# Softmax denominators in a two-layer graph attention kernel: from a ones-matmul per head pair to block transposes, row sums and one small matmul per visit

## The chip, the cores and the metric

The kernel runs on 1 core of one Trainium2 chip. The metric is the device time of one execution in microseconds. Lower is better. The median before the change is 3263.24 us over 3 runs.

## What is computed

64 graphs of 256 nodes, 512 features each, go through two layers of masked attention over the adjacency matrix, each with a layer norm and a ReLU in front and a residual. Layer 0 has 4 heads of 64, layer 1 has 8 heads of 64.

```python
# layer 0
h = maximum(layernorm(x), 0)
q, k, v = split_heads(h @ Wq), split_heads(h @ Wk), split_heads(h @ Wv)
sim = where(adj, q k^T * 64**-0.5, -big);  attn = softmax(sim, over the keys)
x = x + (attn v) @ Wo + bo
# layer 1
h = maximum(layernorm(x), 0);  h = layernorm(h) * gamma + beta
q, k, v = split(h @ w_qkv.T)                      # 8 heads
scores = where(adj | eye, q k^T * 64**-0.5, -1e9)
x = x + (softmax(scores) v) @ w_out.T + b_out
```

What matters here is the softmax. The kernel takes exponentials without subtracting a maximum, multiplies the unnormalised exponentials with v, sums the exponentials over the keys by another way, and multiplies the product with the inverse of that sum. The change is in how that sum is made and how its inverse reaches the place where it is used.

## The kernel before, in words

**Steps and graphs.** A step `s` handles 2 graphs (G = 2), so there are 32 steps. The steps are software-pipelined: while step s is in its layer 1, step s+1 finishes layer 0 and step s+2 starts it. All activations are fp32. The products by weights are 2x2 block products in 7 multiplications (Strassen-like), so that each projection is a "set" of 7 products, numbered n = 1 to 7, taken in the order 1, 6, 5, 2, 7, 3, 4 (`SET`, at the end of the schedule). The result of a product lies in a bank of PSUM and is taken out ("evacuated") by one add of VectorE or one copy of ScalarE (`evacuate`, lines 732 to 749).

**Four shared banks.** `mm_tile` hands out four PSUM banks in turn. `bank_of` (line 783) lets two products share one bank: product 2 accumulates on top of product 1, product 3 on top of 5, and product 4 on top of 7, each after the first of the two was evacuated. The matmuls of product 4 can thus not start before the evacuation of product 7 (line 743) has read the bank.

```python
    SHARED = {2: 1, 4: 7, 3: 5}
```

**Pairs and visits.** Two heads of 64 make a pair (`pr`): 2 pairs in layer 0, 4 in layer 1, 192 in all. A "visit" works on two pairs at once (a few at the edges of the program on one). In the steady state there are three visits in a period of one step, at the places 2.0 (`AT_X`), 4.5 (`AT_Q0`) and 6.2 (`AT_Z`) of a period 6.4 long. A visit closes the two pairs of the visit before it and opens two new ones:

- close: `key_sums` (line 996) multiplies the exponentials, already added over the two halves of the keys by GpSimd (`key_halves`, line 951, result `pd`), with a 128x32 matrix of ones, so that each of four groups of 32 partitions of a bank holds the sums of one (graph, head) repeated 32 times. `invert` (line 1022) takes the reciprocal of that bank (VectorE, 2 instructions of 128x128 for each pair), guards its extremes (line 1032) and issues 8 DMAs for each pair that spread the 32 copies over the 64 partitions of a head (line 1041). `weigh_out` multiplies exponentials and v on TensorE and copies the product out by ScalarE; `normalise` (line 1044) multiplies it by the spread inverses on GpSimd.
- open: `scores` (TensorE), `mask_scores` (VectorE), `exponentials` (ScalarE), `key_halves` (GpSimd).

After each visit TensorE goes on with a projection set: after X the values of layer 1 (`project_v1`), then the output product of layer 0 and the second query/key set of layer 1 ("set B", places 3.5 to 4.5); after Q0 the query/key set of layer 0 and its values; after Z the first query/key set of layer 1 and the output product of layer 1.

**What sets the order.** The order of the instructions on TensorE, VectorE, ScalarE and GpSimd is written out by hand: `at(period, place, fn, ...)` puts every step into a list of events, the list is sorted by place, and each engine gets its instructions in that order. Every engine works through its own queue in order, so an instruction that waits holds all that stand behind it on that engine. The DMAs are issued on SP's queue, in order too, except a few at the edges of the program.

**Lines that the change and the prediction touch.** `norm1` and `norm1_rest` (lines 624 and 641) take the statistics of layer 1's two norms with `bn_stats` (line 576). `turn_blocks` (line 683) transposes 32x32 blocks of the activations on VectorE (line 686), and `move_blocks` (line 693) sends them by 16 DMAs to their places. `neighbours` (line 506) takes a maximum over each row of the adjacency matrix, `neighbours_out` and `neighbours_in` send those by way of DRAM to all partitions.

Of the kernel before, what the change touches and what calls it, by code (L numbers as in the profile page):

```python
# [8 lines left out]
FP = mybir.dt.float32  # L9
# [4 lines left out]
ALU = mybir.AluOpType  # L14
# [301 lines left out]
def fast_path(  # L316
# [19 lines left out]
    nc = tc.nc  # L336
# [3 lines left out]
    G = 2  # L340
# [39 lines left out]
    ones = const.tile([P, 32], FP, name="ones")  # L380
    nc.vector.memset(ones, 1.0)
    mhalf = const.tile([P, NT], FP, name="mhalf")
    nc.gpsimd.memset(mhalf, -0.5)

# [518 lines left out]
    def scores(s, lyr, pr, second):  # L903
        st = S[s]
        qk = st.pop(("qk", lyr, pr))

        sc = [
            [mm_tile([P, NIC, N]) if second and g == 0 else ps_sc.tile([P, NIC, N], FP, name="sc") for e in range(2)]
            for g in range(G)
        ]  # L910
        if second and sums_bank:
            tag = sums_bank.pop()
            banks.remove(tag)
            banks.append(tag)
        for g in range(G):
            for kc in range(NIC):
                for e in range(2):
                    rows = slice(e * DH, (e + 1) * DH)
                    k0 = g * N + kc * P
                    nc.tensor.matmul(  # L920
                        sc[g][e][:, kc, :], qk[rows, 1, k0:k0 + P],
                        qk[rows, 0, g * N:(g + 1) * N], start=True, stop=True,
                    )
# [12 lines left out]
        pd = sm.tile([P, 2, G, N], FP, name="pd", bufs=2)  # L936
        st["sc", lyr, pr], st["p", lyr, pr] = sc, (p, pd)

    def mask_scores(s, lyr, pr, g):

        st = S[s]
        sc, (p, pd), neg = st["sc", lyr, pr][g], st["p", lyr, pr], st[f"n{lyr}"]
        for e in range(2):
            nc.vector.tensor_tensor(p[e][:, g], sc[e], neg[:, :, g, :], ALU.add)  # L944

    def exponentials(s, lyr, pr, g):
        p, pd = S[s]["p", lyr, pr]
        for e in range(2):
            nc.scalar.activation(p[e][:, g], p[e][:, g], AF.Exp, scale=SCALE)  # L949

    def key_halves(s, lyr, pr, e):
        p, pd = S[s]["p", lyr, pr]
        nc.gpsimd.tensor_tensor(pd[:, e], p[e][:, :, 0, :], p[e][:, :, 1, :], ALU.add)  # L953


    def place_values(s, lyr):
        st = S[s]
        tile_o = act.tile([P, NB, HP1, N], FP, name="oT")
        if lyr:
            st["oT1"] = tile_o  # L960
            st["invb"] = [tile_o[:, 3], tile_o[:, 4]]
            st["inv"] = [tile_o[:, 6, i] for i in range(2)]
        else:
            flat = tile_o.rearrange("p b c n -> p (b c) n")
            st["oT0"] = flat[:, :NB].rearrange("p (b c) n -> p b c n", c=HP0)
            st["invb"] = [flat[:, 8:10], flat[:, 10:12]]
            st["inv"] = [flat[:, 12 + i] for i in range(2)]

    def weigh(s, lyr, pr):
        st = S[s]  # L970
        p, _ = st["p", lyr, pr]
        po = ps_sc.tile([P, G, N], FP, name="sc")
        for g in range(G):
            for kc in range(NIC):
                for r0 in range(0, P, 32):
                    nc.tensor.matmul(  # L976
                        po[r0:r0 + 32, g, :],
                        st[f"v{lyr}"][:, g * NIC + kc, pr * P + r0:pr * P + r0 + 32],
                        p[r0 // DH][:, g, kc, :], start=(kc == 0), stop=(kc == NIC - 1),
                    )  # L980
# [15 lines left out]
    def key_sums(s, lyr, prs):  # L996

        st = S[s]
        bank = mm_tile([P, 2, N])
        sums_bank[:] = [banks[-1]] if len(prs) > 1 else []  # L1000
        for i, pr in enumerate(prs):
            _, pd = st["p", lyr, pr]
            st["sums", lyr, pr] = bank[:, i]
            for g in range(G):
                for e in range(2):
                    r0 = 32 * (2 * g + e)
                    nc.tensor.matmul(  # L1007
                        bank[r0:r0 + 32, i, :], ones, pd[:, e, g, :], start=True, stop=True,
                        skip_group_check=True,
                    )  # L1010

    def inverse_places(s, lyr, pr, i):

        if (s, lyr) != (NSTEP - 1, 1):
            return S[s]["inv"][i], S[s]["invb"][i]
        if pr == 0:
            invb = wqk0[:, 6].rearrange("p c k o -> p (c k o)").rearrange("p (g n) -> p g n", g=G)
        else:
            invb = act.tile([P, G, N], FP, name="invb", tag=("n0", "ne", "ab")[pr - 1])
        return bo_b[:, i * N:(i + 1) * N], invb  # L1020

    def invert(s, lyr, pr, i, halves=(0, 1)):
        st = S[s]
        sums = st["sums", lyr, pr]
        if 0 in halves:
            st["place", lyr, pr] = inverse_places(s, lyr, pr, i)
        inv, invb = st["place", lyr, pr]
        for k in halves:
            nc.vector.reciprocal(inv[:, k * P:(k + 1) * P], sums[:, k * P:(k + 1) * P])  # L1029
        if 1 not in halves:  # L1030
            return
        nc.vector.tensor_tensor_reduce(
            out=sums, in0=sums, in1=inv, scale=1.0, scalar=0.0, op0=ALU.add, op1=ALU.max,
            accum_out=extremes[:, units[0]:units[0] + 1],
        )
        units[0] += 1
        for g in range(G):
            for e in range(2):
                r0 = 32 * (2 * g + e)
                for d0 in range(e * DH, (e + 1) * DH, 32):  # L1040
                    nc.sync.dma_start(invb[d0:d0 + 32, g, :], inv[r0:r0 + 32, :])  # L1041
        st["invb", lyr, pr] = invb

    def normalise(s, lyr, pr):
        dst, invb = S[s].pop(("dst", lyr, pr)), S[s].pop(("invb", lyr, pr))
# [27 lines left out]
    def visit(period, w, prev, cur):  # L1073
# [2 lines left out]
        s, lyr, prs = prev  # L1076
        last = (s, lyr) == (NSTEP - 1, 1)
        if prs:
            at(period, w, key_sums, s, lyr, prs)
            if prs[0] == 0 and not last:  # L1080
                at(period, w, place_values, s, lyr)
            for i, pr in enumerate(prs):
                k = i if len(prs) > 1 else pr % 2
                at(period, w + 0.1 * last, invert, s, lyr, pr, k, (0,) if i and not last else (0, 1))
                if not last:
                    at(period, w, weigh_out, s, lyr, pr)
                    at(period, w + (0.55 if len(prs) == 1 else (0.3, 0.75)[i]), normalise, s, lyr, pr)
        for i, pr in enumerate(cur[2]):
            unit = (*cur[:2], pr)
            one = cur[:2] == (0, 0)  # L1090
            at(period, w, scores, *unit, i == 1)
            at(period, w, mask_scores, *unit, 0)
            if i == 1 and len(prs) > 1 and not last:
                at(period, w, invert, s, lyr, prs[1], 1, (1,))
            at(period, w + 1 / 7 if one else w, mask_scores, *unit, 1)
            for g, place in enumerate((0.05, 0.22) if one else ((0.02, 0.03), (0.15, 0.3))[i]):
                at(period, w + place, exponentials, *unit, g)
            for e, place in enumerate((0.23, 0.3) if one else ((0.1, 0.11), (0.35, 0.36))[i]):
                at(period, w + place, key_halves, *unit, e)

    AT_X, AT_C0, AT_QK, AT_Q0, AT_V0, AT_H1, AT_Z = 2.0, 3.0, 3.5, 4.5, 5.5, 6.06, 6.2
    LAST_QK = 4.0
# [22 lines left out]
    visit(-1, 1.54, none, (1, 0, (1,)))  # L1125
    for s in range(NSTEP):

        p = s - 2
# [126 lines left out]
def kernel(tc, *args):  # L1255
# [1 line left out]
    B, N, _ = args[0].shape  # L1257
    P = 128
    with tc.tile_pool(name="guard", bufs=1) as guard:
        extremes = guard.tile([P, B // 2 * 6], FP, name="extremes")  # L1260
# [44 lines left out]
```

## Time and profile before

The numbers are of the one profiled execution, unless said otherwise.

| what | value |
|---|---|
| median of 3 runs (range) | 3263.24 us (3262.0 to 3267.05) |
| the profiled execution's own time | 3261.14 us |
| its span, first to last instruction | 3259.3 us |
| granted TensorE clock | 0.999 |
| TensorE busy (matmul) | 3204.8 us (98%) |
| VectorE busy | 2095.1 us (64%), 3680 instructions |
| ScalarE busy | 1256.6 us (39%) |
| GpSimd busy | 2241.4 us (69%) |
| length of a period in the middle (1413.76 to 1513.97, from one X visit to the next) | 100.2 us |

How to read it: a line of the profile with groups gives the line of the code, the engine, the operation, "output<-input", the shape, how many there were, then the busy time, the mean duration of one in ns, and after the second bar the idle time of the engine just ahead of them with what ended it. A timeline gives the start, the length and the engine of instructions in order, with the idle time ahead of them in brackets. A list of waits gives who waited for whom: the total, the number of times, and the longest.

### The profile page before, as it was taken

What the parts mean: (1) busy time and instruction counts of PE and PEld (TensorE: products, weight loads), DVE (VectorE), ACT (ScalarE), POOL (GpSimd) and SP (SyncE); (2) the same over time, 40 slices, a digit from 0 to 9 for tenths busy, and PEclk for the clock granted to TensorE, in tenths of its full rate; (3) what the DMA queues carried; (4) which work ended last, traced back from release to release, by engine and by line L of the source; (5) the groups of instructions that cost most, each with busy time, mean ns of one, the idle gap of its engine ahead of it and who ended that gap; (6) DMA issues with size and microseconds to landing.
All of it is one profiled execution on the core that took longest, in us unless ns stands there. A gap on an engine that the chain in (4) does not pass through costs nothing.

```text
span 3259.3 us, 59763 instructions
## 1 busy us (share of the span) xinstructions
PE 3204.8 (98%) x22002; PEld 2611.8 (80%) x22002; DVE 2095.1 (64%) x3680; ACT 1256.6 (39%) x2226; POOL 2241.4 (69%) x2124
## 2 busy tenths in 40 slices
PE   9999999999999999999999999999999999999999
PEld 6787878888887888788787888888787888878777
DVE  6656666666666666676666666666666666666665
ACT  4434343343433334343434334343333434343431
POOL 7776776777766767667677677776776766767653
PEclk9999999999999999999999999999999999999999
DMA  4122232232322322223223222222232222322211
GB/s 147 43 85 77 55 85 65 79 82 53 85 69 73 88 60 71 76 67 86 76 55 85 62 82 81 53 84 66 75 86 62 72 70 73 86 72 57 85 31 47
DMA packets 214217, 237.04 MB, mean 73 GB/s; under 512 B 75032, under 2 KB 128416, under 8 KB 213920
## 3 DMA queue, kind: packets, MB, share of 16 engines
q1 hardware_dynamic: 213488, 232.76, 26.0%
q8 instruction: 177, 2.90, 0.4%
q14 instruction: 120, 0.98, 0.1%
q10 hardware_dynamic: 432, 0.40, 0.0%
HBM read 86.12 MB, written 33.62 MB: 37 GB/s over the span
## 4 chain that ended last, share of the span: by engine, by line
PE 66%; POOL 13%; DVE 11%; DMA 5%; SPq 4%; issue 1%; ACT 0%; POOLq 0%; DVEq 0%; ACTq 0%
PE mm L803 26%; PE mm L860 12%; PE sc L976 9%; PE mm L830 7%; PE sc L920 6%; DVE bs L576 5%; SPq L1041 4%; PE mm L1007 3%; POOL xt L498 3%; DMA xt<-in_x_dram 2%; POOL xt L771 2%; POOL n L563 2%; PE mm L920 2%; DVE p L944 2%; DMA oT<-oT 2%
## 5 line engine op out<-in xcount | busy, mean ns | idle before, releaser
L803 PE MATMUL mm<-hT,wqkv 128*128 128x256 f32 x3584 | 795.7, 381 | 31.7 <-DVE qk L743 31.7
L803 PEld LDWEIGHTS mm<-hT,wqkv 128*128 128x128 f32 x3584 | 675.7, 190 | 144.8 <-DVE qk L743 43.7
L953 POOL TENSOR_TENSOR pd<-p 128x512 f32<-128x512 f32 x383 | 479.7, 1274 | 328.1 <-ACT p L949 327.6
L860 PE MATMUL mm<-wo,oT 128*128 128x256 f32 x2632 | 588.3, 381 | 7.6 <-POOL oT L412 5.2
L860 PEld LDWEIGHTS mm<-wo,oT 128*128 128x128 f32 x2632 | 498.9, 191 | 87.1 <-issue 8.8
L1029 DVE RECIPROCAL oT<-mm 128x128 f32<-128x128 f32 x376 | 345.6, 940 | 249.6 <-PE mm L1007 245.6
L949 ACT ACTIVATE p<-p 128x512 f32<-128x512 f32 x766 | 439.6, 626 | 137.0 <-DVE p L944 137.0
L944 DVE TENSOR_TENSOR p<-sc,n 128x512 f32<-128x512 f32 x579 | 363.5, 684 | 113.9 <-PE sc L920 112.5
L844 PE MATMUL mm<-wqkv,hT 128*128 128x256 f32 x1792 | 401.9, 382 | 0.0
L803 PE MATMUL mm<-hT,wqk 128*128 128x256 f32 x1792 | 398.9, 382 | 0.3 <-ACT qk L737 0.2
L803 PEld LDWEIGHTS mm<-hT,wqk 128*128 128x128 f32 x1792 | 338.2, 191 | 56.3 <-issue 10.7
L844 PEld LDWEIGHTS mm<-wqkv,hT 128*128 128x128 f32 x1792 | 335.5, 190 | 53.8 <-issue 10.7
L976 PE MATMUL sc<-p,v 128*32 128x256 f32 x6128 | 350.0, 379 | 1.0 <-issue 1.0
L976 PEld LDWEIGHTS sc<-p,v 128*32 128x32 f32 x6128 | 199.7, 110 | 132.9 <-issue 1.8
L988 ACT COPY oT<-sc 128x512 f32<-128x512 f32 x188 | 109.4, 582 | 500.2 <-PE sc L976 495.3
L1046 POOL TENSOR_TENSOR oT<-oT 128x512 f32<-128x512 f32 x188 | 240.0, 1277 | 83.2 <-DMA oT<-oT 73.5
L920 PE MATMUL sc<-qk 64*128 64x256 f32 x2320 | 292.6, 385 | 0.0
L920 PEld LDWEIGHTS sc<-qk 64*128 64x128 f32 x2320 | 218.7, 186 | 58.8 <-issue 39.6
L771 POOL TENSOR_TENSOR xt<-xt,u 128x512 f32<-128x512 f32 x183 | 228.9, 1272 | 4.4 <-DVE xt L760 1.9
L830 PE MATMUL mm<-wv,hT 128*128 128x256 f32 x1024 | 227.0, 379 | 0.4 <-DVE qk L747 0.4
L830 PEld LDWEIGHTS mm<-wv,hT 128*128 128x128 f32 x1024 | 194.2, 190 | 27.3 <-DVE qk L747 0.7
L592 ACT ACTIVATE h<-h,mr,r 128x512 f32<-128x512 f32 x252 | 184.6, 804 | 0.0
(139 smaller groups left out, 3781.8 us busy)
## 6 DMA issues: line engine op xcount, KB each, us to landing
h<-blocks SPq DMA_DIRECT2D x960, 64.0 KB, 2.0
oT<-oT SPq DMA_DIRECT2D x1504, 32.0 KB, 1.9
xt<-in_x_dram SPq DMA_DIRECT2D x31, 1024.0 KB, 5.8
h<-in_x_dram SPq DMA_DIRECT2D x31, 1024.0 KB, 5.5
out_dram<-xt SPq DMA_DIRECT2D x31, 1024.0 KB, 4.5
ne<-row SPq DMA_DIRECT2D x30, 256.0 KB, 4.7
ad<-in_adj_dram SPq DMA_DIRECT2D x32, 128.0 KB, 8.7
wr<-in_L_gnn_w_qkv_dram SPq DMA_DIRECT2D x3, 1024.0 KB, 9.2
```

Source lines behind the costliest of these rows:

```text
L771: (nc.vector if last else nc.gpsimd).tensor_tensor(r, r, u, ALU.add)
L803: nc.tensor.matmul(bank[:, k, :], w[:, wa, c, k, a * P:(a + 1) * P], st["hT"][:, ba, c, :], start=first and (k, c) == (0, 0), stop=(k, c) ...
L830: nc.tensor.matmul(bank, st["hT"][:, b0 + t // NIC * step, c % HC, i:i + P], wv0[:, c, :], start=(c == 0), stop=(c == NC - 1),)
L844: nc.tensor.matmul(bank[:, t, :], st["hT"][:, ba, c, t * P:(t + 1) * P], wqkv1[:, wa, c, 2, :], start=first and (t, c) == (0, 0), stop=(t, ...
L860: nc.tensor.matmul(bank[:, t, :], oT[:, ba, c, t * P:(t + 1) * P], w[:, wa, c, :], start=first and (t, c) == (0, 0), stop=(t, c) == (NIC - ...
L920: nc.tensor.matmul(sc[g][e][:, kc, :], qk[rows, 1, k0:k0 + P], qk[rows, 0, g * N:(g + 1) * N], start=True, stop=True,)
L944: nc.vector.tensor_tensor(p[e][:, g], sc[e], neg[:, :, g, :], ALU.add)
L949: nc.scalar.activation(p[e][:, g], p[e][:, g], AF.Exp, scale=SCALE)
L953: nc.gpsimd.tensor_tensor(pd[:, e], p[e][:, :, 0, :], p[e][:, :, 1, :], ALU.add)
L976: nc.tensor.matmul(po[r0:r0 + 32, g, :], st[f"v{lyr}"][:, g * NIC + kc, pr * P + r0:pr * P + r0 + 32], p[r0 // DH][:, g, kc, :], start=(kc ...
L1029: nc.vector.reciprocal(inv[:, k * P:(k + 1) * P], sums[:, k * P:(k + 1) * P])
L1046: nc.gpsimd.tensor_tensor(dst, dst, invb, ALU.mult)
```

## The change

Four things change together.

1. Sums over keys. `key_sums` no longer multiplies `pd` by ones. A new step `key_quarters` follows GpSimd's `key_halves` for each pair: VectorE transposes the 32x32 blocks of `pd` (one instruction of 128x1024), then sums along rows (one reduction from 128x1024 to 128x32, into `part`). At the next visit one matmul with `part` as the stationary matrix (128x64 for two pairs) and a 128x32 matrix of four identities (`quarters`) adds the four groups of 32 partitions. Its result is 64x32, each sum once.
2. Inverses. One reciprocal and one guard of 64x32 stand for the two pairs of a visit, in place of four reciprocals of 128x128 and two guards of 128x256. The inverses go to a line in DRAM by one DMA, and come back by two DMAs for each pair, each to 64 partitions with the same 2 KB for all.
3. Buffers. `pd` has one buffer in place of two, so GpSimd's `key_halves` of a pair waits until VectorE has transposed the pair before. `turned_p`, `part` and `inv` have one each.
4. Places. The statistics of layer 1's norms (`norm1`, `norm1_rest`) move from 3.7 to 3.82 and 3.95 to 4.2 to places between 3.79 and 4.37, spread among the evacuations of set B. The guard's array is cleared once at the start.

```diff
     def key_halves(s, lyr, pr, e):
-        p, pd = S[s]["p", lyr, pr]
-        nc.gpsimd.tensor_tensor(pd[:, e], p[e][:, :, 0, :], p[e][:, :, 1, :], ALU.add)
+        st = S[s]
+        p = st["p", lyr, pr]
+        if e == 0:
+            st["pd"] = sm.tile([P, 2, G, N], FP, name="pd", bufs=1)
+        nc.gpsimd.tensor_tensor(st["pd"][:, e], p[e][:, :, 0, :], p[e][:, :, 1, :], ALU.add)
+
+    def key_quarters(s, lyr, prs, i):
+
+        st = S[s]
+        if i == 0:
+            st["part", lyr, prs] = stat.tile([P, 2, 32], FP, name="part", bufs=1)
+        turned = sm.tile([P, 32, 32], FP, name="turned_p", bufs=1)
+        nc.vector.transpose(
+            turned, st.pop("pd").rearrange("p e g (b k) -> p (e g b) k", k=32),
+        )
+        nc.vector.tensor_reduce(st["part", lyr, prs][:, i], turned, axis=mybir.AxisListType.X, op=ALU.add)
...
     def key_sums(s, lyr, prs):
...
-        bank = mm_tile([P, 2, N])
+        part = st.pop(("part", lyr, prs))
+        rows = 32 * len(prs)
+        bank = mm_tile([P, 32])
         sums_bank[:] = [banks[-1]] if len(prs) > 1 else []
-        for i, pr in enumerate(prs):
-            _, pd = st["p", lyr, pr]
-            st["sums", lyr, pr] = bank[:, i]
-            for g in range(G):
-                for e in range(2):
-                    r0 = 32 * (2 * g + e)
-                    nc.tensor.matmul(
-                        bank[r0:r0 + 32, i, :], ones, pd[:, e, g, :], start=True, stop=True,
-                        skip_group_check=True,
-                    )
...
-        for k in halves:
-            nc.vector.reciprocal(inv[:, k * P:(k + 1) * P], sums[:, k * P:(k + 1) * P])
...
+        sums = bank[:rows]
+        nc.tensor.matmul(
+            sums, part[:, :len(prs)].rearrange("p i b -> p (i b)"), quarters, start=True, stop=True
+        )
+        inv = stat.tile([P, 32], FP, name="inv", bufs=1)[:rows]
+        nc.vector.reciprocal(inv, sums)
         nc.vector.tensor_tensor_reduce(
             out=sums, in0=sums, in1=inv, scale=1.0, scalar=0.0, op0=ALU.add, op1=ALU.max,
-            accum_out=extremes[:, units[0]:units[0] + 1],
+            accum_out=extremes[:rows, units[0]:units[0] + 1],
         )
         units[0] += 1
-        for g in range(G):
+        line = dram.tile([len(prs), 2, T], FP, name="line")
+        nc.sync.dma_start(line.rearrange("i e (b q) -> (i e b) q", q=32), inv)
+        for i, pr in enumerate(prs):
+            invb = inverse_place(s, lyr, pr, i if len(prs) > 1 else pr % 2)
             for e in range(2):
-                r0 = 32 * (2 * g + e)
-                for d0 in range(e * DH, (e + 1) * DH, 32):
-                    nc.sync.dma_start(invb[d0:d0 + 32, g, :], inv[r0:r0 + 32, :])
-        st["invb", lyr, pr] = invb
+                nc.sync.dma_start(
+                    invb[e * DH:(e + 1) * DH].rearrange("p g n -> p (g n)"),
+                    bass.AP(tensor=line.tensor, offset=line[i, e, 0:1].offset, ap=[[0, DH], [1, T]]),
+                )
+            st["invb", lyr, pr] = invb
...
+        late = w > AT_Z - 0.01 and period < NSTEP - 2
...
+            if cur[:2] == (1, 0):
+                at(period, w + 0.112, key_quarters, *cur[:2], (0, 1), pr)
+            else:
+                place = 0.31 if one else (0.34, 0.78)[i] if late else (0.29, 0.58)[i]
+                at(period, w + place, key_quarters, *cur, i)
...
-            at(p, ((2.901, 3.041, 3.181, 3.321), (2.99919, 2.99933, 2.99947, 2.99961), (3.7, 3.72, 3.8, 3.82))[edge][k], norm1, s, k)
+            at(p, ((2.901, 3.041, 3.181, 3.321), (2.99919, 2.99933, 2.99947, 2.99961), (3.79, 3.8, 3.94, 3.95))[edge][k], norm1, s, k)
             at(
-                p, ((3.042, 3.182, 3.322, 3.323), (2.99948, 3.2, 3.3, 3.45), (3.95, 4.02, 4.09, 4.2))[edge][k],
+                p, ((3.042, 3.182, 3.322, 3.323), (2.99948, 3.2, 3.3, 3.45), (4.08, 4.22, 4.23, 4.37))[edge][k],
                 norm1_rest, s, k,
             )
```

In VectorE's queue of the changed program, between the masks of a visit and the evacuation of product 7, there now stand, in this order:

- X: evacuation 6; first transpose and sum; evacuation 5; two `turn_blocks`; second transpose and sum; two `turn_blocks`; evacuation 7
- Q0: two `turn_blocks`; evacuation 6; first transpose and sum; two `turn_blocks`; evacuation 5; second transpose and sum; evacuation 7
- Z: first transpose and sum; evacuations 6 and 5; one `bn_stats` with its aggregation; second transpose and sum; one `neighbours`; evacuation 7

The two second inverses of the visit, which stood among the masks, are gone from there. In set B the queue holds evacuation 6, two statistics, evacuation 5, three statistics, evacuation 7, two statistics, evacuation 3, one statistic, evacuation 4; before, it held eight statistics ahead of evacuation 7.

More of the change, by code (lines that the diff above doesn't have):

```diff
@@ L379, in fast_path @@
     nc.vector.memset(onesb, 1.0)
-    ones = const.tile([P, 32], FP, name="ones")
-    nc.vector.memset(ones, 1.0)
+    quarters = const.tile([P, 32], FP, name="quarters")
+    nc.vector.tensor_tensor(quarters, ident[:, 0:32], ident[:, 32:64], ALU.add)
+    for k in (2, 3):
+        nc.vector.tensor_tensor(quarters, quarters, ident[:, 32 * k:32 * (k + 1)], ALU.add)
+    nc.vector.memset(extremes, 0.0)
     mhalf = const.tile([P, NT], FP, name="mhalf")
@@ L935, in scores @@
             p = [sm.tile([P, G, NIC, N], FP, name="p", bufs=4) for _ in range(2)]
-        pd = sm.tile([P, 2, G, N], FP, name="pd", bufs=2)
-        st["sc", lyr, pr], st["p", lyr, pr] = sc, (p, pd)
+        st["sc", lyr, pr], st["p", lyr, pr] = sc, p
     def mask_scores(s, lyr, pr, g):
         st = S[s]
-        sc, (p, pd), neg = st["sc", lyr, pr][g], st["p", lyr, pr], st[f"n{lyr}"]
+        sc, p, neg = st["sc", lyr, pr][g], st["p", lyr, pr], st[f"n{lyr}"]
         for e in range(2):
@@ L946, in exponentials @@
     def exponentials(s, lyr, pr, g):
-        p, pd = S[s]["p", lyr, pr]
+        p = S[s]["p", lyr, pr]
         for e in range(2):
@@ L951, in key_halves @@
     def key_halves(s, lyr, pr, e):
-        p, pd = S[s]["p", lyr, pr]
-        nc.gpsimd.tensor_tensor(pd[:, e], p[e][:, :, 0, :], p[e][:, :, 1, :], ALU.add)
+        st = S[s]
[12 more added lines that the diff above has]
+        nc.vector.tensor_reduce(st["part", lyr, prs][:, i], turned, axis=mybir.AxisListType.X, op=ALU.add)
     def place_values(s, lyr):
@@ L961, in place_values @@
             st["invb"] = [tile_o[:, 3], tile_o[:, 4]]
-            st["inv"] = [tile_o[:, 6, i] for i in range(2)]
         else:
@@ L966, in place_values @@
             st["invb"] = [flat[:, 8:10], flat[:, 10:12]]
-            st["inv"] = [flat[:, 12 + i] for i in range(2)]
     def weigh(s, lyr, pr):
         st = S[s]
-        p, _ = st["p", lyr, pr]
+        p = st["p", lyr, pr]
         po = ps_sc.tile([P, G, N], FP, name="sc")
@@ L1012, in inverse_places @@
[L1012 to L1027, printed above, removed]
-        for k in halves:
-            nc.vector.reciprocal(inv[:, k * P:(k + 1) * P], sums[:, k * P:(k + 1) * P])
-        if 1 not in halves:
-            return
+        sums = bank[:rows]
@@ L1042, in invert, with inverse_place @@
-        st["invb", lyr, pr] = invb
+                nc.sync.dma_start(
[3 more added lines that the diff above has]
+            st["invb", lyr, pr] = invb
+    def inverse_place(s, lyr, pr, i):
+        if (s, lyr) != (NSTEP - 1, 1):
+            return S[s]["invb"][i]
+        if pr == 0:
+            return wqk0[:, 6].rearrange("p c k o -> p (c k o)").rearrange("p (g n) -> p g n", g=G)
+        return act.tile([P, G, N], FP, name="invb", tag=("n0", "ne", "ab")[pr - 1])
@@ L1078, in visit @@
         if prs:
-            at(period, w, key_sums, s, lyr, prs)
             if prs[0] == 0 and not last:
                 at(period, w, place_values, s, lyr)
+            at(period, w, key_sums, s, lyr, prs)
             for i, pr in enumerate(prs):
-                k = i if len(prs) > 1 else pr % 2
-                at(period, w + 0.1 * last, invert, s, lyr, pr, k, (0,) if i and not last else (0, 1))
                 if not last:
@@ L1092, in visit @@
             at(period, w, mask_scores, *unit, 0)
-            if i == 1 and len(prs) > 1 and not last:
-                at(period, w, invert, s, lyr, prs[1], 1, (1,))
             at(period, w + 1 / 7 if one else w, mask_scores, *unit, 1)
@@ L1124, in fast_path @@
     visit(-1, 1.53, none, (1, 0, (0,)))
-    visit(-1, 1.54, none, (1, 0, (1,)))
+    visit(-1, 1.56, none, (1, 0, (1,)))
     for s in range(NSTEP):
@@ L1259 @@
     with tc.tile_pool(name="guard", bufs=1) as guard:
-        extremes = guard.tile([P, B // 2 * 6], FP, name="extremes")
+        extremes = guard.tile([P, B // 2 * 3 + 4], FP, name="extremes")
         ident = guard.tile([P, P], FP, name="ident")
```

## Prediction

> **What bounds the kernel now.** I read the page's busy times first, then TensorE's timeline over one period, then who waited for whom, then VectorE's groups, the timeline of one late evacuation, and the DMAs.
>
> ```profile
> PE 3204.8 (98%) x22002; PEld 2611.8 (80%) x22002; DVE 2095.1 (64%) x3680; ACT 1256.6 (39%) x2226; POOL 2241.4 (69%) x2124
> ```
>
> TensorE has work in 98% of the span, so what counts is how much of its queue goes away and how long it is made to wait. Its timeline around an X visit (start, length):
>
> ```profile
> 1413.76 1.07 PE L1007 MATMUL mm<-pd,ones 128*32 128x256 f32 x16
> 1414.64 3.64 PE L976 MATMUL sc<-p,v 128*32 128x256 f32 x64
> 1418.21 2.00 PE L920 MATMUL sc<-qk 64*128 64x256 f32 x16
> ...
> 1421.87 7.17 PE L844 MATMUL mm<-wqkv,hT 128*128 128x256 f32 x32
> 1428.88 0.61 PE L549 MATMUL mm<-identb,adb 128*128 128x128 bf16 x8
> 1429.32 5.40 PE L844 MATMUL mm<-wqkv,hT 128*128 128x256 f32 x24
> 1434.56 6.46 PE L860 MATMUL mm<-wo,oT 128*128 128x256 f32 x28
> ```
>
> From start to start the sums (L1007) hold TensorE for 0.88 us. The scores follow 3.57 us later and the projection set 3.66 after those; a product of the set takes 1.75 us, and product 4 starts at 1432.81, 10.94 us after the set. TensorE's own list of waits is short:
>
> ```profile
> PE mm L803 <- DVE qk L743: 31.7, 30, 1.8
> ```
>
> Once a period, 30 times, product 4 of set B waits for evacuation 7. VectorE's and TensorE's timelines show why: eight statistics stand ahead of it.
>
> ```profile
> 1451.46 0.18 DVE L577 BATCH_NORM_AGGREGATE mg<-bs 128x2 f32<-128x6 f32 x1
> 1451.56 0.66 DVE L743 TENSOR_TENSOR qk<-mm,qk 128x512 f32<-128x512 f32 x1
> ```
>
> ```profile
> 1452.27 1.99 PE L803 MATMUL mm<-hT,wqkv 128*128 128x256 f32 x8 [0.90 <-DVE qk L743]
> ```
>
> So VectorE at 64% is no bound by its sum, but TensorE stops wherever evacuation 7 ends after product 4's turn. This place decides my forecast. VectorE's groups give the prices:
>
> ```profile
> L944 DVE TENSOR_TENSOR p<-sc,n 128x512 f32<-128x512 f32 x579 | 363.5, 684 | 113.9 <-PE sc L920 112.5
> L1029 DVE RECIPROCAL oT<-mm 128x128 f32<-128x128 f32 x376 | 345.6, 940 | 249.6 <-PE mm L1007 245.6
> L686 DVE STREAM_TRANSPOSE blocks<-h 128x512 f32<-128x512 f32 x240 | 151.9, 681 | 0.0
> L1032 DVE CUSTOM_DVE_ANT_0 mm<-mm,oT 128x256 f32<-128x256 f32 x188 | 81.3, 433 | 10.6 <-ACT oT L988 0.6
> ```
>
> Queued behind each other, four masks or four transposes of 128x512 take 2.48 us, so 0.60 each after the first. The DMAs (KB each, us from issue to landing):
>
> ```profile
> oT<-oT SPq DMA_DIRECT2D x1504, 32.0 KB, 1.9
> ne<-row SPq DMA_DIRECT2D x30, 256.0 KB, 4.7
> row<-any_of SPq DMA_DIRECT2D x30, 2.0 KB, 9.0
> ```
>
> [...] from the last L803 to L1007 the trace has some 0.17 us more than 8 times 0.22. [...]
>
> **The change part by part.**
>
> *Sums on TensorE.* Removed: 96 visits' worth times 0.88 = 84.5 us. Added: 96 matmuls of 32 columns in two fp32 passes. No row shows one. Bounds: 0.1 us [...] and 0.6 us (weight loads of 109 to 190 ns laid bare [...]). I take 0.35[...]: 33.6 us. Gain 51 us (range 27 to 75).
>
> *Statistics of layer 1.* In set B five statistics (two of them pairs of 0.80) stand ahead of evacuation 7 in place of eight. Evacuation 6 can start 3.7 us after the set, +0.6, two statistics 1.65, evacuation 5 0.6, three statistics 2.5 give 9.1; product 7 ends at 8.8. Evacuation 7 is over at 9.7, product 4 is due at 10.6. The wait of 31.7 us goes. The scales that follow come later: the last statistic ends about as the next visit starts, GpSimd's chain (0.20+0.20+1.02+0.19+0.20) 1.85 us later, and ScalarE wants it only after two copies of the weighed values, some 4.5 us into the visit. Hidden.
>
> *VectorE's block steps.* Removed per pair: 2 x 0.94 + 0.43 + 0.14 = 2.45 us. Added per pair: a transpose and a reduction over 1024 elements, by the slope 0.60 per 512 [...], and 0.1 for the wait of the second for the first (statistics and aggregation show 0.73 where 0.62 would do): 2.4 us[...]. Bounds 2.0 and 3.0. The reciprocal and guard of 64x32 cost some 0.5 us a visit. VectorE's total hardly moves, but the work moves from the visit, where TensorE is busy with weighing and scores, into the projection set, ahead of evacuation 7. Count from the set's first matmul. Masks begin 1.16 after the scores and take 4.8, so they end at 2.3 (the inverses among them are gone). Product 6 ends at 3.5; its evacuation can start at 3.75.
> - X: evacuation 6 to 4.35, first pair of steps to 6.75, evacuation 5 to 7.35, two transposes to 8.6, second pair to 11.0, two transposes to 12.2, evacuation 7 to 12.9. Product 4 was due at 10.94: wait 2.0.
> - Q0: evacuation 6 to 4.35, first pair 6.75, two transposes 8.0, evacuation 5 8.6, second pair 11.0, evacuation 7 11.7; due at 10.6: wait 1.15.
> - Z: `pd` is ready at 2.7; first pair to 5.1, evacuations 6 and 5 to 6.35, a statistic to 7.2, second pair 9.6, the maximum 10.2, evacuation 7 10.85: wait 0.3.
>
> In 30 periods 3.45 x 30 = 103 us. Before, evacuation 7 in X started at 1431.31, when its product was done; this cost is new.
>
> *One buffer for `pd`.* GpSimd's second pair (2.5 us) starts at the end of the first transpose, at 5.6 in X and Q0, and ends at 8.1; VectorE asks for it at 8.6. Behind it stand the normalisation, the biases and the sums of oT's blocks; those end at about 14.6 in X, when the output product starts. Cost 0; if the transpose came later by more than 0.5, all of it would show at evacuation 7.
>
> *Inverses through DRAM.* SP issues 5 DMAs a visit for 16. The line is 64 runs of 128 B: between 1.9 (oT) and 9.0 us (row, single elements); I take 2.2. Then two reads a pair of 128 KB, between 1.9 and 4.7, queued: 4.5. Reciprocal done 1.1 us into the visit, issue 0.4, 2.2, two issues 1.4, 3.5: the first pair's inverse lands near 8.6, one us after the set begins. GpSimd wants it 2.6 (X), 4.0 (Q0) and 2.7 (Z) after the set begins, once it has summed the first `pd`. Hidden. SP stands 2 us for the line; behind it are the loads of x and the 16 DMAs of `move_blocks`, which are issued no later than VectorE's transposes allow: in X at 12.3, over by 24, used 33 us after the set. In the tail the last inverses have the 12.3 us of L844 at 3220.91 as cover.
>
> Sum: -51 -32 +103 = +20. The profiled execution took 3261.1 (span 3259.3 and 1.8 around it), so 3281; the median lies 2.1 above it: 3283.
>
> **The rivals.**
> - *Cheap steps, faster.* If a pair of block steps holds VectorE for 2.0 us, X waits 1.2, Q0 0.35, Z 0: 46 us, and the sum is 46-51-32 = -37: 3226. For it: the price is an extrapolation to an unseen size. Against: four transposes in a row fit the slope. It decides below about 2.26 us a pair (each 0.1 is worth some 0.5 us a period).
> - *The small matmul is not small.* [...] it costs 0.6 to 0.9: the 51 us shrink to 0 to 27, giving 3307 to 3334.
> - *The line lands as late as row.* At 9 us the first inverse comes at 8.3 after the set; GpSimd's normalisation holds the second `pd`, that the second pair of steps: evacuation 7 at about 16, 3.5 to 4.3 us more in each visit, +340: 3620. It begins to decide when the inverse comes later than 4.3. Against: 128 B runs are not single elements, and oT's land in 1.9.
> - *No change to speak of*: waits of 2.6 to 3.0 us a period and a matmul of 0.35 cancel: within 6.5 us of 3263.
>
> **How the numbers follow.** Forecast (waits exceed the gain) 0.49, at 3283, own range 3270 to 3310; costly matmul 0.08; late line 0.05; within 0.2%, which is about what a measurement of this kernel can tell from no change, 0.11; cheap steps 0.27. Slower 0.62, same 0.11, faster 0.27. The range leaves out the late line, the worst of the costly matmul, and the lower part of the cheap steps: 3222 to 3332.
>
> **What would show it.** L1007's place taken by a 32-column group, its successor 0.3 to 0.4 us later; the block steps at 1.2 us each; TensorE waiting for evacuation 7 (now in v1 and in both qk sets) about 2, 1.2 and 0.3 us; the wait of set B gone; hardly any wait of the normalisation on a DMA. I am wrong if TensorE waits under 2.7 us a period for VectorE, or if GpSimd waits long for the line.

## The result, and the profile after

The changed kernel takes 3306.91 us (median of 4 runs, 3305.09 to 3307.41), the kernel before, measured beside it, 3264.55 (4 runs). The ratio is 1.0129, with a 95% interval of 1.0111 to 1.0146: 42 us slower, where 20 were forecast. The profiled execution took 3307.41 us with a span of 3305.6, 46.3 more than the span before.

The page's busy times for the changed kernel:

```profile
PE 3171.7 (96%) x20660; PEld 2580.4 (78%) x20660; DVE 2150.6 (65%) x3590; ACT 1250.5 (38%) x2226; POOL 2235.8 (68%) x2124
```

TensorE has 33 us less work in a span that is 46 us longer. Its timeline from the Q0 visit to the next X visit, with the X set before it (start, length; in brackets the idle time just ahead and who ended it):

```profile
1446.68 7.17 PE L847 MATMUL mm<-wqkv,hT 128*128 128x256 f32 x32
...
1459.64 1.99 PE L847 MATMUL mm<-wqkv,hT 128*128 128x256 f32 x8 [1.83 <-DVE v L746]
1461.47 6.46 PE L863 MATMUL mm<-wo,oT 128*128 128x256 f32 x28
1467.76 12.25 PE L806 MATMUL mm<-hT,wqkv 128*128 128x256 f32 x56
1479.94 0.30 PE L1018 MATMUL mm<-quarters,part 128*64 128x32 f32 x2
1480.17 3.66 PE L990 MATMUL sc<-p,v 128*32 128x256 f32 x64
...
1487.42 10.76 PE L806 MATMUL mm<-hT,wqk 128*128 128x256 f32 x48
1499.28 1.97 PE L806 MATMUL mm<-hT,wqk 128*128 128x256 f32 x8 [1.10 <-DVE qk L746]
1501.08 7.07 PE L833 MATMUL mm<-wv,hT 128*128 128x256 f32 x32
...
1515.56 10.63 PE L806 MATMUL mm<-hT,wqkv 128*128 128x256 f32 x48
1526.71 1.97 PE L806 MATMUL mm<-hT,wqkv 128*128 128x256 f32 x8 [0.53 <-DVE qk L746]
1528.52 12.25 PE L863 MATMUL mm<-wo,oT 128*128 128x256 f32 x56
```

The sums' matmul holds TensorE 0.23 us (1479.94 to 1480.17) where the old one held it 0.88. Set B, at 1467.76, runs through. But the X set now stops ahead of product 4, and so do the sets of Q0 and Z. TensorE's list of waits (total, times, longest) says the same:

```profile
PE mm L847 <- DVE v L746: 56.5, 31, 2.2
PE mm L806 <- DVE qk L746: 49.6, 61, 1.1
...
PE mm L806 <- DVE qk L744: 5.4, 1, 5.4
PE mm L469 <- ACT wqkv L474: 4.4, 1, 4.4
```

VectorE's queue in the Q0 set shows what stands ahead of evacuation 7 (L746), due when product 7 is done:

```profile
1491.24 0.69 DVE L742 TENSOR_TENSOR qk<-mm,qk 128x512 f32<-128x512 f32 x1 [0.23 <-PE mm L806]
1491.85 1.24 DVE L966 STREAM_TRANSPOSE turned_p<-pd 128x1024 f32<-128x1024 f32 x1
1493.12 1.22 DVE L969 TENSOR_REDUCE part<-turned_p 128x32 f32<-128x1024 f32 x1
1494.26 1.30 DVE L689 STREAM_TRANSPOSE blocks<-h 128x512 f32<-128x512 f32 x2
1495.48 0.65 DVE L744 TENSOR_TENSOR qk<-mm,qk 128x512 f32<-128x512 f32 x1
1496.05 1.23 DVE L966 STREAM_TRANSPOSE turned_p<-pd 128x1024 f32<-128x1024 f32 x1
1497.32 1.22 DVE L969 TENSOR_REDUCE part<-turned_p 128x32 f32<-128x1024 f32 x1
1498.45 0.68 DVE L746 TENSOR_TENSOR qk<-mm,qk 128x512 f32<-128x512 f32 x1
```

From 1491.24 on VectorE has no gap. The set began at 1487.42, so evacuation 7 ends 11.71 us later; the forecast had 11.7.

**Where the 46.3 us lie.** From one X visit to the next a period takes 101.60 us, where it took 100.42 (29 periods: 34.1 us). The first full X visit starts at 219.69 instead of 208.71 (11.0 us). The tail gives the rest, a little over 1 us.

The start of the program has two stops of its own. In TensorE's timeline, at the first visits:

```profile
51.43 1.12 PE L469 MATMUL mm<-ident,wr 128*128 128x128 f32 x4 [4.37 <-ACT wqkv L474]
52.34 3.62 PE L806 MATMUL mm<-hT,wqk 128*128 128x256 f32 x8
...
104.01 6.01 PE L806 MATMUL mm<-hT,wqkv 128*128 128x256 f32 x16 [5.36 <-DVE qk L744]
```

VectorE's and ScalarE's timelines give the chain of the first one: VectorE waits for `pd`, then takes the two block steps, and only then the copy of the weights (L474) that ScalarE's copy follows. The second is alike: from 96.16 to 102.47 VectorE takes the block steps of both pairs, waiting for `pd` ahead of each, and only then evacuations 6 and 5 (L744), for which TensorE waits.

```profile
48.15 1.25 DVE L966 STREAM_TRANSPOSE turned_p<-pd 128x1024 f32<-128x1024 f32 x1 [2.66 <-POOL pd L958]
49.42 1.22 DVE L969 TENSOR_REDUCE part<-turned_p 128x32 f32<-128x1024 f32 x1
50.56 0.41 DVE L474 COPY wqkv<-mm 128x256 f32<-128x256 f32 x1
```

### The profile page after: what moved, and what is told of

It is laid out like the page before. It is cut to its first block, busy times and chain, and to the rows that moved or that the text cites. A ratio compares the mean times of both kernels' runs of the same rounds, so it can differ in the third digit from the quotient of the medians.

```text
span 3305.6 us, 54389 instructions
## 1 busy us (share of the span) xinstructions
PE 3171.7 (96%) x20660; PEld 2580.4 (78%) x20660; DVE 2150.6 (65%) x3590; ACT 1250.5 (38%) x2226; POOL 2235.8 (68%) x2124
## 4 chain that ended last, share of the span: by engine, by line
PE 59%; DVE 20%; POOL 8%; issue 4%; DMA 4%; ACT 3%; SPq 1%; ACTq 0%; DVEq 0%; POOLq 0%
PE mm L806 19%; PE mm L863 16%; DVE turned_p L966 6%; PE sc L990 6%; PE mm L833 5%; PE sc L923 5%; PE mm L847 5%; DVE part L969 4%; DVE blocks L689 3%; ACT hT L714 2%; POOL pd L958 2%; DMA xt<-in_x_dram 2%; DMA out_dram<-xt 1%; PE mm L923 1%; DVE qk L742 1%
## 5 line engine op out<-in xcount | busy, mean ns | idle before, releaser
L946 DVE TENSOR_TENSOR p<-sc,n 128x512 f32<-128x512 f32 x579 | 363.2, 683 | 343.5 <-PE sc L923 342.0
L847 PE MATMUL mm<-wqkv,hT 128*128 128x256 f32 x1792 | 414.5, 387 | 56.5 <-DVE v L746 56.5
L806 PE MATMUL mm<-hT,wqk 128*128 128x256 f32 x1792 | 412.1, 387 | 33.2 <-DVE qk L746 33.2
L990 PEld LDWEIGHTS sc<-p,v 128*32 128x32 f32 x6128 | 190.4, 110 | 118.7 <-issue 0.6
L1002 ACT COPY oT<-sc 128x512 f32<-128x512 f32 x188 | 109.0, 582 | 445.2 <-PE sc L990 443.2
L966 DVE STREAM_TRANSPOSE turned_p<-pd 128x1024 f32<-128x1024 f32 x192 | 235.6, 1227 | 23.9 <-POOL pd L958 23.8
L969 DVE TENSOR_REDUCE part<-turned_p 128x32 f32<-128x1024 f32 x192 | 234.2, 1220 | 6.6
```

The lines of the kernel that those rows point to most:

```text
L806: nc.tensor.matmul(bank[:, k, :], w[:, wa, c, k, a * P:(a + 1) * P], st["hT"][:, ba, c, :], start=first and (k, c) == (0, 0), stop=(k, c) ...
L847: nc.tensor.matmul(bank[:, t, :], st["hT"][:, ba, c, t * P:(t + 1) * P], wqkv1[:, wa, c, 2, :], start=first and (t, c) == (0, 0), stop=(t, ...
L966: nc.vector.transpose(turned, st.pop("pd").rearrange("p e g (b k) -> p (e g b) k", k=32),)
L969: nc.vector.tensor_reduce(st["part", lyr, prs][:, i], turned, axis=mybir.AxisListType.X, op=ALU.add)
L990: nc.tensor.matmul(po[r0:r0 + 32, g, :], st[f"v{lyr}"][:, g * NIC + kc, pr * P + r0:pr * P + r0 + 32], p[r0 // DH][:, g, kc, :], start=(kc ...
```

## The experiments

Each edit is against the changed kernel unless it says otherwise; times are medians, intervals 95% of the ratio to the kernel before (3263.2 us beside runs 1 to 4, 3264.0 beside runs 5 to 7 and the first of run 8, 3261.8 beside the rest). My theory: the order in VectorE's queue costs the time. Rivals: the price of the steps, the trip through DRAM, GpSimd's single `pd`, the transfers of the blocks.

**1. The second pair of block steps behind evacuation 7.**

```diff
-                place = 0.31 if one else (0.34, 0.78)[i] if late else (0.29, 0.58)[i]
+                place = 0.31 if one else (0.34, 0.93)[i] if late else (0.29, 0.73)[i]
```

> The changed kernel with one edit: the second pair of block steps of every visit stands behind evacuation 7 in VectorE's queue instead of ahead of it. Theory 'order' (TensorE loses the time where product 4 waits for evacuation 7): the waits of 2.1, 1.5 and 0.8 us a period go, about 4.3 x 29 = 125 us, so some 3180 us, and the list of TensorE's waits has next to nothing from evacuation 7. Theory 'inverses' (the way through DRAM holds GpSimd or SP and these hold the rest): no change, 3300 to 3310.

3229.87 us, ratio 0.9898 (0.9882 to 0.9915). The same work in another order is 77 us faster, so the order is the main cost. But 50 us of what was expected are missing, and the waits say where:

```profile
PE sc L923 <- DVE p L946: 23.3, 30, 0.8
PE mm L863 <- DVE xt L763: 19.1, 29, 0.7
```

Z's scores now take 4.70 us for 3.65, and the output product stops for 0.76 (start to start). Runs 6, 8 and 9 come back to them.

**2. The spread of the statistics alone, in the kernel before.** Only the places of `norm1` and `norm1_rest` are those of the changed kernel.

> The kernel before with one part of the change alone: the statistics of layer 1's norms at the new places. Theory 'order': the wait of 31.7 us for evacuation 7 of set B goes and nothing comes in its place: 3230 to 3233 us. If the later statistics delay the next set's input, the gain is smaller or none: 3255 to 3270.

3223.05 us, ratio 0.9878 (0.9862 to 0.9895). The 40 us gained exceed the 31.7 us that the list of waits showed. This stop costs more than its idle time: in the period that the prediction shows, set B takes 13.35 us from start to start, where this run has 12.18, which is 1.17 us for the 0.90 on the list. The 30 sets B of the kernel before take 13.51 us in the mean, so that 1.33 x 30 = 40 us go, the whole gain.

**3. No line in DRAM.** The reads take rows of `x` in place of the line.

```diff
-        nc.sync.dma_start(line.rearrange("i e (b q) -> (i e b) q", q=32), inv)
...
-                    bass.AP(tensor=line.tensor, offset=line[i, e, 0:1].offset, ap=[[0, DH], [1, T]]),
+                    bass.AP(tensor=x.tensor, offset=x.offset + (2 * i + e) * T, ap=[[0, DH], [1, T]]),
```

> The changed kernel without the DMA that writes the inverses to DRAM; the two reads of each pair take rows of x instead, so they wait for no inverse and the products are not normalised rightly. Theory 'order': the trip is hidden, 3300 to 3310 us. Theory 'inverses': what the trip costs comes back, 3270 us or less.

3345.75 us, ratio 1.0255 (1.0238 to 1.0272): a miss, and not a clean experiment. With no inverse to depend on, the reads of Z moved ahead of the 16 DMAs of `move_blocks` in SP's queue, and waited there for their place to be free: on SP's list the reads wait for GpSimd's normalisations 62 times, 717.4 us in all and 22.0 at the longest. The blocks came late, and ScalarE waited:

```profile
1423.87 2.93 ACT L714 ACTIVATE hT<-h,gb 128x512 f32<-128x512 f32 x4 [1.47 <-DMA h<-blocks]
1426.71 1.05 ACT L1002 COPY oT<-sc 128x512 f32<-128x512 f32 x2
```

Z's scores need the banks that the second line frees. Over all periods they take 4.95 us in the mean for 3.65. The run says nothing on the trip; run 5 does.

**4. The first visits' block steps moved.** `place` is 0.665 in place of 0.31 for the second unit of step 0; step 1's two pairs go behind evacuations 6 and 3 of their set, and since `pd` has one buffer, GpSimd's sums for the second of them (`key_halves`) move behind the first pair's block steps:

```diff
-                at(period, w + place, key_halves, *unit, e)
+                if unit == (1, 0, 1):
+                    at(0, 0.291 + 0.001 * e, key_halves, *unit, e)
+                else:
+                    at(period, w + place, key_halves, *unit, e)
...
-                at(period, w + 0.112, key_quarters, *cur[:2], (0, 1), pr)
+                at(0, (0.29, 0.9)[pr], key_quarters, *cur[:2], (0, 1), pr)
```

> The changed kernel with the first visits' block steps at other places: the one of step 0's second pair behind the copy of layer 1's weights and evacuation 6, those of step 1's two pairs behind evacuation 6 and behind evacuation 3 of the first layer 1 set. The steady periods are untouched. Theory: of the 46 us that the span grew by, 11 came before the first full period, through two stops of TensorE of 4.4 and 5.4 us and the slow matmuls after them; these go, 3294 to 3298 us. If the edges don't matter: 3305 to 3309.

3297.4 us, ratio 1.0105 (1.0088 to 1.0121). 9.5 us are gained, and the steady waits are unchanged. The first full X visit starts at 212.09 where it started at 219.69: 7.6 us, so the two stops are most of the 11.0 us lost at the start.

**5. Two trips.** The line is copied to a second line in DRAM, and the reads take that.

```diff
-        nc.sync.dma_start(line.rearrange("i e (b q) -> (i e b) q", q=32), inv)
+        first = dram.tile([len(prs), 2, T], FP, name="first")
+        nc.sync.dma_start(first.rearrange("i e (b q) -> (i e b) q", q=32), inv)
+        nc.sync.dma_start(line, first)
```

> Changed kernel, the inverses go to one line in DRAM, from there to a second line, and are read from that: one more DMA and one more landing of 1.7 us or more, 2.2 us with its issue. Theory (the trip is hidden; in X and Q0 the inverse lands 2.8 and 3.9 us before GpSimd asks for it, in Z 1.8): 3305 to 3318, the upper end if Z's normalisation becomes late by 0.4. Rival (the trip is on the path now and is a part of what was missed): 2.2 us in three visits a period, +130 to +200.

3400.68 us, ratio 1.04 (1.0374 to 1.0425): the theory's 3318 at most is missed. One reason is that I gave the second trip 2.2 us; its landing alone takes 3.0 us in the median. In X the reads are issued 8.56 us after the visit starts, where the changed kernel has 2.83, since the load of `x` now goes ahead of them: 5.73 us later. GpSimd's timeline in X:

```profile
1491.93 1.27 POOL L1051 TENSOR_TENSOR oT<-oT 128x512 f32<-128x512 f32 x1 [3.77 <-DMA oT<-line]
1493.16 2.49 POOL L958 TENSOR_TENSOR pd<-p 128x512 f32<-128x512 f32 x2
```

So in X some 2 us of the delay (5.73 - 3.77) are hidden. One trip is hidden, as the page of the changed kernel says too (the normalisation waited 6.5 us in all):

```profile
L1049 POOL TENSOR_TENSOR oT<-oT 128x512 f32<-128x512 f32 x188 | 239.9, 1276 | 6.5 <-DMA oT<-line 6.5
```

Past that, the late inverse holds the second `pd` and that holds evacuation 7: TensorE's stop in X grew from 1.83 to 3.38 in this period (to 3.4 in the mean: 104.2 us in 31 stops). This is the rival of the late line, with its mechanism, at a delay that the change does not have.

**6. Spread steps.** Runs 1 and 4 together, and two orders mended:

```diff
-                place = 0.31 if one else (0.34, 0.78)[i] if late else (0.29, 0.58)[i]
+                place = (0.31, 0.665)[pr] if one else (0.34, 0.93)[i] if late else (0.28 if w < 2.1 else 0.29, 0.73)[i]
...
-                at(p, AT_Q0 + (0.15, 0.16, 0.29, 0.3)[k], turn_blocks, s, 1, NORM1[k])
+                at(p, AT_Q0 + (0.15, 0.16, 0.286, 0.287)[k], turn_blocks, s, 1, NORM1[k])
...
-            at(p, AT_Q0 + 0.31, move_blocks, s)
+            at(p, AT_Q0 + 0.288, move_blocks, s)
```

> Changed kernel with three moves: every second block-step pair behind evacuation 7 (as in the run that did only this), the first visits' block steps moved as in the run of the edges, and two orders mended: in X the first pair goes ahead of evacuation 6, in Q0 the two turn_blocks go ahead of the first pair. Theory (only the order of VectorE's queue and what hangs on it costs time; the run with the second pair behind evacuation 7 had 1.93 us a period of new stops, 0.76 at the output product, 1.04 in Z, 0.13 in Q0): 3230 - 9.5 for the edges - 1.9 x 30 = 3164, between 3155 and 3185. Rival (those stops come from GpSimd's single buffer and from the DMAs, which the two moves don't touch): 3215 to 3225.

3167.04 us, ratio 0.9699 (0.9683 to 0.9715): a hit, and faster than all other kernels here. The page's busy line, and the longest of its TensorE waits:

```profile
PE 3141.0 (99%) x20660; PEld 2581.2 (82%) x20660; DVE 2158.7 (68%) x3590; ACT 1250.6 (39%) x2226; POOL 2237.8 (71%) x2124
```

```profile
PE mm L723 <- ACT h L621: 7.2, 3, 6.6
PE mm L863 <- POOL oT L415: 5.9, 1, 5.9
```

VectorE does the same work as in the changed kernel, and no wait on TensorE's list recurs once a period. Q0's set still takes 12.32 us for the 12.19 of before.

**7. The old statistics in the changed kernel.** The places of `norm1` and `norm1_rest` are those of before.

> Changed kernel with the statistics of layer 1 back at their old places. Theory (set B's stop of 1.17 us a period comes back and adds to the rest): 3307 + 35 = 3342. Rival (the spread gives nothing beside the block steps, since the scales it delays are then waited for elsewhere): 3307 to 3315.

3315.62 us, ratio 1.0154 (1.0137 to 1.0171). Only 8.7 us come back, nearer to the rival, for another reason than the rival's. VectorE's first statistic of set B, in the kernel before and then in this run:

```profile
1443.96 0.70 DVE L576 BATCH_NORM_STATS2 bs<-xt 128x6 f32<-128x512 f32 x1 [2.22 <-POOL xt L771]
```

```profile
1475.99 0.69 DVE L579 BATCH_NORM_STATS2 bs<-xt 128x6 f32<-128x512 f32 x1 [1.35 <-POOL xt L774]
```

Set B starts at 1440.85 in the one and at 1473.75 in the other: the statistic comes 3.11 us into it before, 2.24 here. While TensorE stops in X, GpSimd goes on and gains a lead of 0.87 us, and set B is shorter by just that (12.48 for 13.35; over the periods 12.46 for 13.48 in the mean). That the lead comes from X's stop is read from these lines; no run has the old statistics without that stop. Here a stop early in the period pays for part of a later one; the terms do not simply add.

**8. Half a sum.** The price of a step: the reduction covers half of the blocks, the other columns of `part` keep a constant, and each pair is some 0.53 us shorter (an estimate: in the changed kernel's trace the one other long reduction, of 128x512, takes 676 ns and a mask of 128x512 takes 683, where this sum over 128x1024 takes 1220). Run twice: with the pool of score banks as it is, then with the four banks handed out in turn.

```diff
-        nc.vector.tensor_reduce(st["part", lyr, prs][:, i], turned, axis=mybir.AxisListType.X, op=ALU.add)
+        nc.vector.tensor_reduce(st["part", lyr, prs][:, i, :16], turned[:, :16], axis=mybir.AxisListType.X, op=ALU.add)
```

> Changed kernel, the row sum covers 16 of the 32 row blocks (128x512 elements, about 0.67 to 0.69 us, for 128x1024); the other half of part keeps a constant, so half of the sums are left out. Each pair of block steps is 0.53 us shorter; all else stays. Theory (each step's time ahead of evacuation 7 is paid by TensorE one for one until the stop is gone): X 2.02 to 0.96, Q0 1.42 to 0.36, Z 0.71 to 0, together 2.83 us x 30 = 85: 3222. Rival (evacuation 7 waits for GpSimd's second pd, not for VectorE's own time): 3280 to 3307.

3262.53 us, ratio 0.9996 (0.9988 to 1.0005), between both. The stops shrank (X 1.03, Q0 0.43, Z none), but Z's scores took 1.04 us longer:

```profile
1492.00 1.56 PE L927 MATMUL sc<-qk 64*128 64x256 f32 x10
1493.91 0.91 PE L927 MATMUL sc<-qk 64*128 64x256 f32 x5 [0.35 <-DVE p L950]
```

One matmul of these scores now waits for VectorE's masks (L950), while in the changed kernel the scores run through. My reading: the pool had given it a bank that is still being masked, not one that ScalarE has just copied. Run 1's list shows the same wait (L946). Run 3's does not: there the scores wait for ScalarE's copy (L1002, 23.9 us, 30 times).

> The run with half of each row sum (half of the sums left out), and nothing else but that the four score banks are handed out strictly in turn. In that run the pool had given one of Z's second scores a bank that VectorE still masks, where the changed kernel gives the bank that ScalarE has just copied; Z's scores took 4.70 us for 3.66. Theory (this choice of bank, not the block steps, cost 1.04 us a period): 3262.5 - 1.04 x 29 = 3232, within 6. Rival (Z's scores wait for ScalarE's copies whatever the bank): 3256 to 3263.

3232.34 us, ratio 0.991 (0.9894 to 0.9927): a hit. The scores run through, so the choice of bank cost the 1.04 us:

```profile
1477.67 2.00 PE L927 MATMUL sc<-qk 64*128 64x256 f32 x16
```

So some 0.53 us less in a pair is worth 75 us. X and Q0 each give 0.79 us a period of the 1.06 that the estimate takes out, Z its whole stop.

**9. Run 1 with the banks in turn.**

> The run with every second block-step pair behind evacuation 7, with the four score banks in turn. Theory (its Z stop of 1.04 us a period was the pool's choice of bank; the output product's 0.76 stays): 3230 - 1.04 x 29 = 3200, within 6. Rival (the Z stop came from the transfers of the blocks, which land as late as before): 3225 to 3231.

3210.23 us, ratio 0.9844 (0.9828 to 0.986): 20 of the 30 us. From Z to X a period now takes 31.85 us in some periods and up to 33.45 in others. In the latter ScalarE's copies are late, some because the moved blocks land late (17 waits, 11.8 us). Both theories hold a part; run 6, which transposes the blocks of Q0 earlier, has 31.85 throughout.

**10. X alone.** Only X's pairs are moved as in run 6; banks in turn.

> Changed kernel with X's block steps alone moved (first pair ahead of evacuation 6, second behind evacuation 7), Q0 and Z as they are, score banks in turn (the same choice as the changed kernel has). Theory (each set pays its own stop): X's 2.10 us a period go, 3307 - 2.1 x 29 = 3246, within 6; Q0 keeps 1.10 and Z 0.53 of waits. Rival (X's stop gave GpSimd a lead that kept set B free; without it set B stops by some 0.9 as before): 3270.

3242.8 us, ratio 0.994 (0.9924 to 0.9957): a hit. X's stop is gone, Q0 keeps 1.10 and Z 0.55, and set B stays free.

## Why the prediction was wrong

The direction and the mechanism held: waits of product 4 for evacuation 7, in the three sets named. Two terms of the sum failed: the stops were put too low, and the first visits had no term at all. By its steps, per period where it recurs (times from start to start; a mean is that of the 29 periods from the first full X visit on):

| step | forecast | measured |
|---|---|---|
| sums on TensorE, 3 visits | -0.53 each | -0.65 each (0.88 to 0.23); the products behind them +0.02 each |
| set B | -1.06 | -1.30 in the mean (13.48 to 12.18) |
| stop in X | 2.0 | 2.10 (set 12.69 to 14.79), 2.20 in the mean |
| stop in Q0 | 1.15 | 1.47 (12.19 to 13.66) |
| stop in Z | 0.3 | 0.76 (12.19 to 12.95) |
| a period | +0.80 | +1.18 |
| start and tail | -4 (some 6 further visits at the same gain) | +12.2 |

- *Block steps: right.* 2.4 us a pair were taken, and 2.45 measured:

```profile
L966 DVE STREAM_TRANSPOSE turned_p<-pd 128x1024 f32<-128x1024 f32 x192 | 235.6, 1227 | 23.9 <-POOL pd L958 23.8
L969 DVE TENSOR_REDUCE part<-turned_p 128x32 f32<-128x1024 f32 x192 | 234.2, 1220 | 6.6
```

The cheap steps fall with this, and the costly small matmul with its 0.23 us. The rival of the costly matmul named 3307 to 3334, and 3307 is what was measured, but what that rests on did not happen. The 0.17 us more that the prediction reads ahead of L1007 stand behind a matmul group that had just waited; before the other two visits, where nothing had waited, the trace of the kernel before has no such excess (1474.49 to 1481.49, 32 matmuls in 7.00 us, 0.22 each). The bounds of 0.1 and 0.6 us for the small matmul, its 0.35, and the rival's 0.6 to 0.9 were the author's estimates.
- *Stops: mis-sized.* "In 30 periods 3.45 x 30 = 103 us": measured are 4.33 us in most periods and 4.42 in the mean, so some 133. Evacuation 7 itself ended where it was put: 12.90 for 12.9 in X, 11.71 for 11.7 in Q0, 11.01 for 10.85 in Z. What was missed lies around it. Product 4 is due after six of seven products, 10.44 us in Q0 and Z, not at the 10.6 taken. It starts 0.06 to 0.15 us after the evacuation's end. And the restarted product takes 1.80 to 1.83 us to the next group's start, not 1.75. Together these are 0.1 us more than forecast in X, 0.3 in Q0 and 0.5 in Z, and two periods in which X's set took 16.3 us add 0.1 to the mean: some +29 us in 30 periods, against some 16 us more gain than forecast from the sums and set B.
- *The start: left out.* "-51 -32 +103 = +20" has no term for the first visits: the places of the block steps, and the cost of 0 for `pd`'s one buffer, were worked out for X, Q0 and Z only. In the first visits VectorE waits for `pd` (2.66 and 4.61 us) with the weights' copy or the evacuations behind it: 11.0 us before the first full X visit, of which run 4 has 7.6 back.
- *Statistics: right in the kernel before, not in what the spread adds beside the block steps.* Set B's stop is gone, and run 2 shows that the spread does that alone. But in run 7, without the spread, 1.02 of the 1.30 us are gone too.
- *Inverses through DRAM: right.* The line lands 1.7 us after its issue (2.2 taken), the reads at 3.7. The reciprocal of 64x32 takes 0.34 us and the guard 0.19, with 0.13 for its accumulator (some 0.5 taken for all). Run 5 shows some 2 us of a further delay hidden in X; the forecast's own times (lands 1.0 us into the set, wanted at 2.6) left 1.6.
- *One buffer in the steady state: right.* Of the 0.5 us that the forecast left over, some 0.3 were there: in run 8, with each pair some 0.53 us shorter, two sets gave 0.79 of the estimated 1.06, and VectorE then waits for the second `pd` (its waits for `pd` rise from 39 to 98, from 23.8 to 35.9 us).

Left open: how much of run 3's loss comes from the late blocks and how much from the choice of bank; and two buffers for `pd`, which no run here has.

## What to carry to other kernels

When work moves to an engine with idle time, place it by what stands behind it in that engine's queue: here the same instructions gave 1.013 with both pairs of block steps ahead of the one evacuation that TensorE waits for, 0.990 with the second pair of each visit behind it, and 0.970 with the first visits and two orders mended as well. Work out the due time by start-to-start times, give each stop its restart (1.80 to 1.83 us here, for a product of 1.75), and take the first visits as a case of their own. Before a run's time is taken as an answer, compare its waits with those of the kernel that it was made from, since a dropped dependency can move a DMA (run 3) and a pool can pick another buffer (run 8, where that cost 1.04 us a period).

## What was not expected of the hardware

After the two long stops TensorE runs slower. The changed kernel in four stretches; the clock granted is the number behind POOL:

```profile
46.00:51.00 5.00, 1.06 (x11) 0.72 (x9) 2.82 (x4) 0.62 (x2) 5.00 (x5) 0.97 0.17 52
51.00:56.00 5.00, 4.57 (x15) 3.67 (x16) 0.57 (x1) 1.93 (x4) 4.27 (x4) 0.50 0.00 0
58.00:62.00 4.00, 4.00 (x35) 3.22 (x28) 0.00 (x0) 1.99 (x6) 1.50 (x2) 1.00 0.22 65
...
104.00:110.00 6.00, 5.99 (x18) 4.89 (x19) 3.97 (x8) 0.00 (x0) 5.12 (x6) 0.61 0.11 17
```

After 4.37 us of idle time the clock is 0.50, and eight matmuls take 3.62 us, where eight at 59.27 take 1.89, with the clock at 1.00 again; after 5.36 us it is 0.61. In run 5 the stop of 3.38 us in X is followed by 0.67, and from 1506.00 to 1510.00 the clock is 1.00 again. The length of a stop alone was not shown to divide the two cases. Of the 29 stops in X of the changed kernel from the first full X visit on, 27 last 1.82 or 1.83 us, and the product behind each takes 1.99 or 2.00 us; after the one shown above the clock is 1.00 (1459.60 to 1461.60). One of 2.18 us (at 1865.92) is followed by a product of 3.21 us, at 0.60, and one of only 1.86 us by 0.53 (the matmuls behind the stop, then the stretch):

```profile
849.05 3.50 PE L847 MATMUL mm<-wqkv,hT 128*128 128x256 f32 x8 [1.86 <-DVE v L746]
```

```profile
849.30:852.90 3.60, 3.60 (x10) 2.86 (x10) 0.61 (x2) 0.00 (x0) 3.60 (x5) 0.53 0.39 96
```

What sets a stop of 1.86 us apart from one of 1.83 no run shows.

So a stop can cost its own time and time in the work behind it: 3.50 us in place of 1.99 for one product. Run 5 lost 93 us: its list has 55 us more of waits for evacuation 7 than the changed kernel's (160.7 for 106.1), and its granted clock over the span is 0.981 for 0.996. That the slower clock makes up most of the rest is argued; no run shows it apart.
